# The first MLP of a four-layer attention kernel written by token, with its norm and modulation on ACT from the fifth group on

## The chip, the cores and the metric

The kernel runs on one core of a Trainium2 chip. A core has five engines that run beside each other, each with its own instruction queue: PE (matrix multiply; its loads of stationary operands are listed apart as PEld), DVE (vector), ACT (scalar, with the activation functions), POOL (a slower vector engine[...]) and SP, which here only issues DMAs. Instructions of one engine start in program order; engines wait for each other through semaphores. Matrix products land in PSUM, everything else lives in SBUF. The metric is the time of one execution on the device in microseconds (us). The kernel before takes 1635.25 us, the median of 3 runs (1635.12 to 1635.38).

## The reference, cut to what matters

`x` is 128 batches of 64 tokens of 128 channels in float32, `ctx` has the same shape, `cond` is one vector of 128 per batch. Four layers follow each other. Layers 0 and 2 have a self-attention, a cross-attention to `ctx` and an MLP; layer 1 is a cross-attention, layer 3 a routed mixture of experts. The change is in the MLP of layer 0 and in the statistics of `ctx` that layers 1 and 2 need:

```python
mod = silu(cond) @ adaln_w + adaln_b          # six vectors of 128 per batch
sh_sa, sc_sa, g_sa, sh_ff, sc_ff, g_ff = split(mod, 6)
...
xm = layernorm(x, 1e-6) * (1 + sc_ff) + sh_ff # the MLP's input
h  = gelu(xm @ fc1_w + fc1_b)                 # 512 hidden channels
x  = x + g_ff * (h @ fc2_w + fc2_b)
# layer 1: layernorm(x, 1e-5), layernorm(ctx, 1e-5);  layer 2: layernorm(ctx, 1e-6)
```

## The kernel before, in words

The 8192 tokens are cut into 16 groups of 512 tokens (8 batches). A group's `x` stays in SBUF for the whole kernel as `xs[s]`, 128 tokens per partition row in four tiles. All order is written out by hand: the program order of the Python calls is the order in each engine's queue, and so in SP's queue of DMAs.

**Attention** (`attend`) is a software pipeline of half groups. Each `step(k)` emits the scores of one half (PE, then on DVE the row maximum L477 and the subtraction L479, 2.3 us each), the transposes and exponentials of the half before, the weighted sum of the half before that, and pieces of `prepare` (norm, keys, queries, values of groups to come) and `finish` (normalise, project, add to `x`).

**The first MLP** (`mlp` called with `mv_out=x_mv`) runs 18 turns. For group `j`, `turn(j)` emits, in this order: the norm of group j+2 (`norm`: five POOL instructions, L361 and four of L364); four products into the 512 hidden channels (`hidden`, PE L676, and Gelu on ACT, L677), each followed by one of the four products out of them for group j-1 (`output`, L682); between the second and third of these `enter`, which transposes the normed group j+1 on PE (L334), multiplies it with its scale on DVE (L339) and adds its shift on POOL (L340); `measure`, the statistics of group j+3 on DVE (L312, L314) and their inverse root on POOL (L321, L322); then `beside(j)`, which loads and measures context group j (`measure_context`: one DMA, eight DVE instructions, seven POOL instructions L654 to L657) and computes one piece of the tables of later layers; last `gate(j-1)` (bias and gate on DVE, L707) and `leave(j-2)`, which transposes the product back to tokens (PE, L715), adds it to `x` (DVE, L716) and takes the statistics of the new `x` for layer 1.

The product `py` of the first MLP comes out with channels on partitions, hence the transposes of L715. The MLP of layer 2 is called with `by_token=True`: there the hidden activations are the stationary operand (L692), `py` has tokens on partitions, and bias and gate come from a tile `gt` that two DMAs per group broadcast from a small table in DRAM (`gate_table`, `gate_tile`); POOL adds the bias part (L698), DVE multiplies with the gate (L702) and adds (L703).

**The seams.** `into_mlp` interleaves the MLP's first five pieces (`heads`) and its first turns with the last steps of the attention before. At the other end, five turns are followed by pieces of the next attention's `prepare` (`second` in `stages`), which add norms and masked keys (L364, L403, L436) to POOL's queue; the last products of group 15 and the first scores of the next attention come after them.

Of the kernel before, what the change touches and what calls it, by code (L numbers as in the profile page):

```python
# [9 lines left out]
F32 = mybir.dt.float32  # L10
AF = mybir.ActivationFunctionType
# [48 lines left out]
def tile_kernel(ctx: ExitStack, tc: tile.TileContext, a: dict, out: bass.AP):  # L60
# [5 lines left out]
    def const(shape, name):  # L66
        return cp.tile(shape, F32, tag=name, name=name)
# [231 lines left out]
    def by_batch(t):  # L299
        return t.rearrange("p (b l) -> p b l", b=NB)  # L300


    ctx_rs = {eps: const([P, NST, TT], f"ctx_rs{i}") for i, eps in enumerate((1e-5, 1e-6))}
    ctx_nb = {eps: const([P, NST, TT], f"ctx_nb{i}") for i, eps in enumerate((1e-5, 1e-6))}


    x_mv = const([P, NST, TT, 2], "x_mv")
# [70 lines left out]
    def prepare(pools, at):  # L378
# [16 lines left out]
        if cross:  # L395
            cn = c
            if layer != "L0c":
                cn = pool.tile([P, TT, P], F32, tag="cn", name="cn", bufs=1)
                for t in range(TT):
                    rs, nb = (v[eps][:, s, t : t + 1] for v in (ctx_rs, ctx_nb))  # L400

                    if layer == "L1c" or s == 0:
                        G.tensor_scalar(cn[:, t, :], c[:, t, :], rs, nb, ALU.mult, ALU.add)  # L403
                    else:
                        S.activation(cn[:, t, :], c[:, t, :], AF.Identity, bias=nb, scale=rs)
# [238 lines left out]

    def measure_context(s):
        pool = pools[0]
        c = pool.tile([P, TT, P], F32, tag="cm", name="c")
        nc.sync.dma_start(c, ctx_d[s])  # L650
        mv = pool.tile([P, TT, 2], F32, tag="mvc", name="mvc")
        stats(pool, c, mv)
        nmu = pool.tile([P, TT], F32, tag="nmuc", name="nmuc")
        G.tensor_scalar(nmu, mv[:, :, 0], -1.0, 0.0, ALU.mult, ALU.add)  # L654
        for eps in ctx_rs:
            rs = power(ctx_rs[eps][:, s], mv, eps)
            G.tensor_tensor(ctx_nb[eps][:, s], nmu, rs, ALU.mult)  # L657

    def mlp(wmod, w1, b1, w2, b2, beside, mv_out=None, by_token=False):

        pool, psum = pools[:2]

        def measure(d):
            d["mv"], d["rs"] = stats_of(pool, xs[d["s"]], 1e-6)

        def norm(d):
            d["xn"] = normed_by_pool(pool, xs[d["s"]], d["mv"], d["rs"], "xn")

        def enter(d):
            d["xm"] = modulated(pool, transposed(psum, d["xn"]), wmod, 4, 3, d["s"])  # L670

        def hidden(d, f):
            if f == 0:
                d["h"] = pool.tile([P, 4, NT], F32, tag="e", name="h")
            ph = pools[2].tile([P, 512], F32, tag="ph", name="ph")
            T.matmul(ph, w[w1][:, 0, ts(f, P)], d["xm"], start=True, stop=True)  # L676
            S.activation(d["h"][:, f, :], ph, AF.Gelu_apprx_tanh, bias=col(b1, f))  # L677

        def output(d, f):
            if f == 0:  # L680
                d["py"] = pools[3].tile([P, 512], F32, tag="py", name="py")
            T.matmul(d["py"], w[w2][:, f, :], d["h"][:, f, :], start=f == 0, stop=f == 3)  # L682

        def gates_of(d):
            d["gt"] = gate_tile(pool, d["s"], w2)

        def output_by_token(d, t):
# [9 lines left out]
        def bias_by_token(d):  # L697
            G.tensor_tensor(xs[d["s"]], xs[d["s"]], d["gt"][:, :, 1, :], ALU.add)  # L698

        def leave_by_token(d):  # L700
            y = pool.tile([P, TT, P], F32, tag="y", name="y")
            V.tensor_tensor(y, d["py"], d["gt"][:, :, 0, :], ALU.mult)  # L702
            V.tensor_add(xs[d["s"]], xs[d["s"]], y)  # L703

        def gate(d):
            d["y"] = pool.tile([P, NT], F32, tag="y", name="y")
            V.scalar_tensor_tensor(  # L707
                by_batch(d["y"]), by_batch(d["py"]), col(b2), mod(wmod, 5, d["s"]),
                ALU.add, ALU.mult,
            )  # L710

        def leave(d):
            pt = psum.tile([P, 512], F32, tag="mm", name="psB")
            for t in range(TT):
                T.transpose(pt[:, ts(t, P)], d["y"][:, ts(t, P)], ident)  # L715
            V.tensor_add(xs[d["s"]], xs[d["s"]], pt.rearrange("p (t c) -> p t c", t=TT))  # L716
# [16 lines left out]

        def turn(j):
            out = output_by_token if by_token else output
            go(norm, j + 2)
            go(hidden, j, 0)
            go(out, j - 1, 0)
            go(hidden, j, 1)
            go(out, j - 1, 1)  # L740
            go(enter, j + 1)
            go(measure, j + 3)
            if by_token:
                go(bias_by_token, j - 1)
            go(hidden, j, 2)
            go(out, j - 1, 2)
            if 0 <= j < NST:
                beside(j)
            go(hidden, j, 3)
            go(out, j - 1, 3)  # L750
            if by_token:
                go(leave_by_token, j - 1)
                go(gates_of, j)
            else:
                go(gate, j - 1)
                go(leave, j - 2)

        return heads, [lambda j=j: turn(j) for j in range(NST + 2)]


# [412 lines left out]
    def stages():  # L1173
# [4 lines left out]
            pools, [attention_of(s, layer) for layer in ("L1c", "L2s", "L2c") for s in groups]  # L1178
        )

        def beside_0(j):
            measure_context(j)
            if j < len(later_tables):
                later_tables[j]()

        def beside_2(j):
# [2 lines left out]

        heads_0, turns_0 = mlp(  # L1190
            "L0_xcond_adaln_w", "L0_xcond_fc1_w", "L0_xcond_fc1_b", "L0_xcond_fc2_w",
            "L0_xcond_fc2_b", beside_0, mv_out=x_mv,
        )
        heads_2, turns_2 = mlp(
            "L2_xcond_W_mod", "L2_xcond_W_mlp1", "L2_xcond_b_mlp1", "L2_xcond_W_mlp2",
            "L2_xcond_b_mlp2", beside_2, by_token=True,
        )
        last = 5

# [32 lines left out]
            f()  # L1232
        first_mods[2]()
        n = last + 2 + len(heads_0)
        for f in steps_1[6:-n]:
            f()
        rest = into_mlp(steps_1, heads_0, turns_0)
        second = [(0, 1, 2), (0,), (1, 0), (0, 0, 1, 2), (0, 1, 1, 2, 0, 0, 3, 3)]
        n_ = len(second)
# [66 lines left out]
```

## Time and profile before

| | us |
|---|---|
| median of 3 runs | 1635.25 |
| the profiled execution: time of the run | 1632.74 |
| its span from first to last instruction | 1631.0 |
| first MLP, first hidden product (turn 0) | at 408.07 |
| turns 0 to 3 | 408.07 to 443.44 |
| turns 4 to 13 | 443.44 to 523.53 |
| turns 14 to 16 with the next attention's first pieces | 523.53 to 557.06 |
| second MLP, turn 0 starts | at 1136.03 |

The profile lists for each instruction its start, its length, and, in brackets, how long its engine had stood idle before it and which instruction of which engine ended that. PE is busy for nearly the whole span, so a change counts by what it takes from PE's queue or adds to it, and by the gaps in it. The granted PE clock is 0.996 over the span. There are three stretches of 3.4 us at half clock, one near the start, one from 557.4 us (the end of the first MLP) and one from 1130.8 us.

### The profile page before, as it was taken

The numbers are of one execution on the slowest core, as the hardware profiler recorded it, in microseconds if no ns is written. First come the engines' busy times: TensorE is split into PE (matmuls) and PEld (weight loads), VectorE is DVE, ScalarE is ACT, GpSimd is POOL, SyncE is SP. The second block draws the span as 40 slices with busy tenths as digits, with TensorE's granted clock in tenths as the row PEclk, the third lists the DMA queues.
The fourth block names the chain that finished last, engine by engine and source line by source line (L and its number), as shares of the span: only waits on it lengthen the run. The fifth ranks groups of instructions, "written<-read, shape, count | busy, mean of one in ns | idle before, by whom it ended". The sixth has DMA issues, their size and how long they took to land.

```text
span 1631.0 us, 64964 instructions
## 1 busy us (share of the span) xinstructions
PE 1577.1 (97%) x27842; PEld 1089.0 (67%) x27842; DVE 1296.5 (79%) x2430; ACT 1037.2 (64%) x1710; POOL 1084.7 (67%) x1818
## 2 busy tenths in 40 slices
PE   6999999998999899999999999998999999999998
PEld 4677777776554477777777677776777666666665
DVE  7999999998576688899999999997454576666666
ACT  5788777776333587788888888886334544444443
POOL 6688776776799888986778876665876333333322
PEclk9999999999999999999999999999999999999999
DMA  7334443322202022211333532222433111111100
GB/s 208 82 82 97 108 121 91 89 80 62 61 27 59 27 58 62 63 47 49 85 94 82 116 95 63 73 57 57 120 91 78 30 39 37 40 33 35 34 11 20
DMA packets 146783, 112.71 MB, mean 69 GB/s; under 512 B 36357, under 2 KB 125247, under 8 KB 146495
## 3 DMA queue, kind: packets, MB, share of 16 engines
q1 hardware_dynamic: 146288, 108.53, 25.8%
q8 instruction: 219, 3.59, 1.0%
q14 instruction: 69, 0.57, 0.1%
q10 hardware_dynamic: 207, 0.03, 0.0%
HBM read 83.99 MB, written 14.02 MB: 60 GB/s over the span
## 4 chain that ended last, share of the span: by engine, by line
PE 79%; DVE 13%; ACT 3%; POOL 3%; issue 1%; DMA 0%; SPq 0%; POOLq 0%; DVEq 0%; ACTq 0%
PE sc L470 10%; PE pp L495 9%; PE po L512 7%; PE ph L1063 6%; PE ph L1064 6%; DVE e L479 6%; DVE mx L477 6%; PE ph L676 6%; PE po L1094 5%; PE psT L334 5%; PE pk L428 5%; PE py L555 4%; PE py L692 3%; PE pvv L451 3%; PE pq L441 3%; PE py L682 2%
## 5 line engine op out<-in xcount | busy, mean ns | idle before, releaser
L499 ACT ACTIVATE eT<-pp 128x1024 f32<-128x1024 f32 x320 | 329.8, 1030 | 159.4 <-PE pp L495 159.3
L477 DVE TENSOR_REDUCE mx<-sc 128x32 f32<-128x2048 f32 x160 | 366.6, 2291 | 58.6 <-PE sc L470 58.6
L479 DVE TENSOR_TENSOR e<-sc,mx 128x2048 f32<-128x2048 f32 x160 | 366.6, 2291 | 5.4
L495 PEld LDWEIGHTS pp<-ident,e 64*128 64x128 f32 x5120 | 184.9, 139 | 140.7 <-ACT eT L499 44.8
L495 PE MATMUL pp<-ident,e 64*128 64x64 f32 x5120 | 228.7, 229 | 7.1 <-DVE e L479 4.7
L364 POOL TENSOR_SCALAR xn<-x,nmu,rs 128x128 f32<-128x128 f32 x508 | 224.7, 456 | 13.3
L436 POOL TENSOR_SCALAR kbd<-kT,mask 128x512 f32<-128x512 f32 x316 | 213.2, 693 | 26.9 <-ACT kT L430 24.5
L549 POOL TENSOR_TENSOR oT<-o,rb 128x512 f32<-128x512 f32 x80 | 102.3, 1278 | 164.5 <-DMA rb<-recs 63.6
L470 PE MATMUL sc<-kbd,qT 32*64 32x256 f32 x5120 | 180.5, 389 | 16.4 <-DVE e L479 15.4
L677 ACT ACTIVATE h<-ph,vec 128x512 f32<-128x512 f32 x128 | 87.4, 688 | 154.8 <-PE ph L676 154.6
L512 PE MATMUL po<-eT,vbd 128*32 128x64 f32 x10240 | 178.4, 221 | 1.1 <-issue 1.0
L1070 ACT ACTIVATE h<-h 128x512 f32<-128x512 f32 x112 | 70.6, 630 | 148.1 <-DVE h L1066 129.2
L512 PEld LDWEIGHTS po<-eT,vbd 128*32 128x32 f32 x10240 | 151.9, 110 | 14.0 <-issue 1.6
L322 POOL TENSOR_TENSOR rs<-rs,nhalf 128x4 f32<-128x4 f32 x128 | 130.4, 1019 | 10.7
L470 PEld LDWEIGHTS sc<-kbd,qT 32*64 32x64 f32 x5120 | 98.1, 131 | 53.1 <-issue 20.2
L1066 DVE TENSOR_TENSOR h<-ph,ab 128x512 f32<-128x512 f32 x112 | 77.0, 688 | 56.2 <-PE ph L1064 56.1
L312 DVE BATCH_NORM_STATS2 st<-x 128x6 f32<-128x128 f32 x512 | 110.5, 278 | 0.8 <-DMA x<-in_x_dram 0.3
L1099 DVE SCALAR_TENSOR_TENSOR acc<-po,pr,acc 128x128 f32<-128x128 f32 x192 | 67.3, 350 | 44.1 <-PE po L1094 39.5
L1063 PE MATMUL ph<-nx,w 128*128 128x512 f32 x192 | 99.9, 602 | 0.0
L520 ACT COPY o<-po 128x512 f32<-128x512 f32 x160 | 95.8, 598 | 5.2 <-PE po L512 3.6
L1064 PE MATMUL ph<-u,w_ev 128*128 128x512 f32 x192 | 98.0, 592 | 0.0
L1094 PEld LDWEIGHTS po<-w_2o,h 128*128 128x128 f32 x768 | 92.1, 192 | 8.7 <-issue 8.4
(261 smaller groups left out, 2849.8 us busy)
## 6 DMA issues: line engine op xcount, KB each, us to landing
rb<-recs SPq DMA_DIRECT2D x80, 256.0 KB
c<-in_ctx_dram SPq DMA_DIRECT2D x64, 256.0 KB
o<-o SPq DMA_DIRECT2D x320, 32.0 KB
gt<-gate_L_xcond_sa_proj_w SPq DMA_DIRECT2D x32, 256.0 KB
gt<-gate_L_xcond_W_proj SPq DMA_DIRECT2D x32, 256.0 KB
gt<-gate_L_xcond_W_mlp SPq DMA_DIRECT2D x32, 256.0 KB
x<-in_x_dram SPq DMA_DIRECT2D x16, 256.0 KB
ctxT<-cm SPq DMA_DIRECT2D x16, 256.0 KB
```

The source lines that it names most:

```text
L322: G.tensor_tensor(rs, rs, nhalf, ALU.pow)
L364: engine.tensor_scalar(xn[:, t, :], src[:, t, :], nmu[:, t : t + 1], rs[:, t : t + 1], ALU.add, ALU.mult)
L436: (V if at.get("first") else G).tensor_scalar(kbd[:, j], by_batch(kT), mask[:, j : j + 1], 1.0, ALU.mult, ALU.mult)
L470: T.matmul(sc[ts(h, L), g, ts(t2, 256)], qT[ts(g, 32), ts(b, L)], kbd[ts(g, 32), :, b, :], start=True, stop=True,)
L477: V.tensor_reduce(mx, sc.rearrange("p g (m k) -> p (g m) k", k=L), AX.X, ALU.max)
L479: V.tensor_tensor(e, sc.rearrange("p g (m k) -> p (g m) k", k=L), mx.unsqueeze(2).broadcast_to([P, 32, L]), ALU.subtract,)
L495: T.transpose(pp[:, h, ts(4 * g2 + 2 * i + t2, L)], e6[ts(h, L), 2 * gg + g2, t2, i], ident[ts(h, L), ts(h, L)],)
L499: S.activation(eT[:, gg], pp, AF.Exp, scale=HD ** -0.5)
L512: T.matmul(po[ts(g, 32), i, ts(2 * t2 + h, L)], at["vbd"][:, 4 * u + 2 * t2 + h, 2 * g + i, :], e7[:, g // 2, h, g % 2, i, t2, :], start=T ...
L1063: T.matmul(ps, wn, d["nx"], start=True, stop=False)
L1064: T.matmul(ps, we, d["u"], start=False, stop=True)
L1094: T.matmul(po[:, ex, :], d[q][:, ts(t, P)], k3["w_2o"][:, q, :], start=r == 0, stop=r == 1)
```

## The change

Six things are edited.

1. The first MLP is written like the second: `output`, `bias`, `leave` by token. The variants with channels on partitions go (`gate`, the transposes of L715). `leave(j-1)` follows the products of group j-1 in the same turn, and the statistics for layer 1 follow it. Each turn issues the two DMAs of `gate_tile` for the next group, which wait behind what SP has queued before.
2. The table that these read is made in steps 7 and 9 of the first attention, one DVE product in the one, two PE transposes, one DVE copy and a DMA in the other.
3. For groups 4 to 15 (`by_act=4`), `norm` is two small POOL instructions (the bias `-mean/std`) and four ACT instructions, and `enter` uses `modulated_by_batch`, eight ACT instructions on 64 columns each, instead of one DVE and one POOL instruction.
4. Contexts are loaded ahead: groups 0 and 1 beside the last two `heads`, then group s+2 right after the statistics of group s are issued.
5. No context is measured in turns 0 to 3; turns 4, 6, 8 and 10 measure two each, turns 5, 7, 9 and 11 to 15 one.
6. One context's POOL part is five instructions instead of seven: both powers are one instruction over 8 columns, and so are both products.

```diff
     def measure_context(s):
         pool = pools[0]
-        c = pool.tile([P, TT, P], F32, tag="cm", name="c")
-        nc.sync.dma_start(c, ctx_d[s])
         mv = pool.tile([P, TT, 2], F32, tag="mvc", name="mvc")
-        stats(pool, c, mv)
+        stats(pool, measured[s], mv)
+        load_context(s + 2)
         nmu = pool.tile([P, TT], F32, tag="nmuc", name="nmuc")
         G.tensor_scalar(nmu, mv[:, :, 0], -1.0, 0.0, ALU.mult, ALU.add)
-        for eps in ctx_rs:
-            rs = power(ctx_rs[eps][:, s], mv, eps)
-            G.tensor_tensor(ctx_nb[eps][:, s], nmu, rs, ALU.mult)
+        rs = ctx_rs[:, s]
+        for i, eps in enumerate(ctx_eps):
+            G.tensor_scalar(rs[:, i], mv[:, :, 1], eps, 1.0, ALU.add, ALU.mult)
+        G.tensor_tensor(rs, rs, nhalf.unsqueeze(1).broadcast_to([P, 2, TT]), ALU.pow)
+        G.tensor_tensor(ctx_nb[:, s], nmu.unsqueeze(1).broadcast_to([P, 2, TT]), rs, ALU.mult)
...
         def norm(d):
-            d["xn"] = normed_by_pool(pool, xs[d["s"]], d["mv"], d["rs"], "xn")
+            if d["s"] < by_act:
+                d["xn"] = normed_by_pool(pool, xs[d["s"]], d["mv"], d["rs"], "xn")
+                return
+            nb = pool.tile([P, TT], F32, tag="nmuxn", name="nb")
+            G.tensor_scalar(nb, d["mv"][:, :, 0], -1.0, 0.0, ALU.mult, ALU.add)
+            G.tensor_tensor(nb, nb, d["rs"], ALU.mult)
+            d["xn"] = pool.tile([P, TT, P], F32, tag="xn", name="xn")
+            for t in range(TT):
+                S.activation(
+                    d["xn"][:, t, :], xs[d["s"]][:, t, :], AF.Identity,
+                    bias=nb[:, t : t + 1], scale=d["rs"][:, t : t + 1],
+                )
 
         def enter(d):
-            d["xm"] = modulated(pool, transposed(psum, d["xn"]), wmod, 4, 3, d["s"])
+            f = modulated if d["s"] < by_act else modulated_by_batch
+            d["xm"] = f(pool, transposed(psum, d["xn"]), wmod, 4, 3, d["s"])
...
         def turn(j):
-            out = output_by_token if by_token else output
             go(norm, j + 2)
             go(hidden, j, 0)
-            go(out, j - 1, 0)
+            go(output, j - 1, 0)
             go(hidden, j, 1)
-            go(out, j - 1, 1)
+            go(output, j - 1, 1)
             go(enter, j + 1)
             go(measure, j + 3)
-            if by_token:
-                go(bias_by_token, j - 1)
+            go(bias, j - 1)
             go(hidden, j, 2)
-            go(out, j - 1, 2)
+            go(output, j - 1, 2)
             if 0 <= j < NST:
                 beside(j)
             go(hidden, j, 3)
-            go(out, j - 1, 3)
-            if by_token:
-                go(leave_by_token, j - 1)
-                go(gates_of, j)
-            else:
-                go(gate, j - 1)
-                go(leave, j - 2)
+            go(output, j - 1, 3)
+            go(leave, j - 1)
+            go(gates_of, j)
...
+        contexts = iter(groups)
+
         def beside_0(j):
-            measure_context(j)
+            for _ in range(0 if j < 4 else 2 if j in (4, 6, 8, 10) else 1):
+                measure_context(next(contexts))
             if j < len(later_tables):
                 later_tables[j]()
...
-        for f in steps_1[6:-n]:
-            f()
+        table = in_two(
+            gate_table, "L0_xcond_adaln_w", "L0_xcond_fc2_w", 5, col("L0_xcond_fc2_b")
+        )
+        for k, f in enumerate(steps_1[6:-n]):
+            f((), [table[k // 2]] if k in (1, 3) else ())
+        for s in range(2):
+            heads_0[3 + s] = lambda s=s, f=heads_0[3 + s]: (f(), load_context(s))
```

More of the change, by code (lines that the diff above doesn't have):

```diff
@@ L300, in by_batch @@
         return t.rearrange("p (b l) -> p b l", b=NB)
-    ctx_rs = {eps: const([P, NST, TT], f"ctx_rs{i}") for i, eps in enumerate((1e-5, 1e-6))}
-    ctx_nb = {eps: const([P, NST, TT], f"ctx_nb{i}") for i, eps in enumerate((1e-5, 1e-6))}
+    ctx_eps = (1e-5, 1e-6)
+    ctx_rs, ctx_nb = (const([P, NST, 2, TT], n) for n in ("ctx_rs", "ctx_nb"))
     x_mv = const([P, NST, TT, 2], "x_mv")
@@ L399, in prepare @@
                 for t in range(TT):
-                    rs, nb = (v[eps][:, s, t : t + 1] for v in (ctx_rs, ctx_nb))
+                    rs, nb = (v[:, s, ctx_eps.index(eps), t : t + 1] for v in (ctx_rs, ctx_nb))
                     if layer == "L1c" or s == 0:
@@ L643, in attention_of, with load_context, mlp @@
         )
+    measured = {}
+    def load_context(s):
+        if s < NST:
+            measured[s] = pools[0].tile([P, TT, P], F32, tag="cm", name="c")
+            nc.sync.dma_start(measured[s], ctx_d[s])
     def measure_context(s):
         pool = pools[0]
-        c = pool.tile([P, TT, P], F32, tag="cm", name="c")
-        nc.sync.dma_start(c, ctx_d[s])
         mv = pool.tile([P, TT, 2], F32, tag="mvc", name="mvc")
-        stats(pool, c, mv)
+        stats(pool, measured[s], mv)
+        load_context(s + 2)
         nmu = pool.tile([P, TT], F32, tag="nmuc", name="nmuc")
         G.tensor_scalar(nmu, mv[:, :, 0], -1.0, 0.0, ALU.mult, ALU.add)
-        for eps in ctx_rs:
-            rs = power(ctx_rs[eps][:, s], mv, eps)
-            G.tensor_tensor(ctx_nb[eps][:, s], nmu, rs, ALU.mult)
-    def mlp(wmod, w1, b1, w2, b2, beside, mv_out=None, by_token=False):
+        rs = ctx_rs[:, s]
[3 more added lines that the diff above has]
+        G.tensor_tensor(ctx_nb[:, s], nmu.unsqueeze(1).broadcast_to([P, 2, TT]), rs, ALU.mult)
+    def mlp(wmod, w1, b1, w2, beside, mv_out=None, by_act=NST):
         pool, psum = pools[:2]
@@ L677, in hidden, with output @@
             S.activation(d["h"][:, f, :], ph, AF.Gelu_apprx_tanh, bias=col(b1, f))
[L679 to L682, printed above, removed]
         def gates_of(d):
             d["gt"] = gate_tile(pool, d["s"], w2)
-        def output_by_token(d, t):
+        def output(d, t):
             if t == 0:
@@ L695, in output_by_token, with bias, leave @@
                 )
-        def bias_by_token(d):
+        def bias(d):
             G.tensor_tensor(xs[d["s"]], xs[d["s"]], d["gt"][:, :, 1, :], ALU.add)
-        def leave_by_token(d):
+        def leave(d):
             y = pool.tile([P, TT, P], F32, tag="y", name="y")
@@ L703, in leave_by_token @@
             V.tensor_add(xs[d["s"]], xs[d["s"]], y)
[L705 to L716, printed above, removed]
             if mv_out is not None:
@@ L1191, in stages @@
             "L0_xcond_adaln_w", "L0_xcond_fc1_w", "L0_xcond_fc1_b", "L0_xcond_fc2_w",
-            "L0_xcond_fc2_b", beside_0, mv_out=x_mv,
+            beside_0, mv_out=x_mv, by_act=4,
         )
@@ L1195, in stages @@
             "L2_xcond_W_mod", "L2_xcond_W_mlp1", "L2_xcond_b_mlp1", "L2_xcond_W_mlp2",
[L1196 removed]
+            beside_2,
         )
```

## The prediction, made before the change was run

> **What bounds the kernel now.** I read the page first (which engine is full), then the first MLP by stretches, then PE's order of time there for its gaps, then the queues behind the gaps. PE is the full engine:
>
> ```profile
> PE 1577.1 (97%) x27842; PEld 1089.0 (67%) x27842; DVE 1296.5 (79%) x2430; ACT 1037.2 (64%) x1710; POOL 1084.7 (67%) x1818
> ```
>
> In the windows of turns 4 to 13 of the first MLP and of turns 2 on of the second (length, then busy us of PE, PEld, DVE, ACT, POOL), PE stands still for 0.8 of 80.09 us, but POOL is 91% busy; the second MLP, already by token, has no PE gap at all:
>
> ```profile
> 443.44:523.53 80.09, 79.27 (x255) 39.70 (x255) 54.70 (x272) 27.51 (x40) 72.60 (x153) 1.00 0.15 43
> 1149.57:1265.40 115.83, 115.83 (x723) 86.97 (x722) 56.55 (x189) 44.03 (x64) 83.99 (x137) 1.00 0.39 98
> ```
>
> PE's gaps (in brackets) are POOL's modulation arriving late at turns 2, 4 and 14, and at the end the first scores of the next attention:
>
> ```profile
> 425.14 1.13 PE L676 MATMUL ph<-xm,L_xcond_fc_w 128*128 128x512 f32 x2 [2.62 <-POOL xm L340]
> ...
> 443.44 1.13 PE L676 MATMUL ph<-xm,L_xcond_fc_w 128*128 128x512 f32 x2 [0.76 <-POOL xm L340]
> ...
> 523.53 1.12 PE L676 MATMUL ph<-xm,L_xcond_fc_w 128*128 128x512 f32 x2 [0.81 <-POOL xm L340]
> ...
> 557.06 1.77 PE L470 MATMUL sc<-kbd,qT 32*64 32x256 f32 x32 [2.48 <-DVE e L479]
> ```
>
> POOL's queue, one context block: 3.4 us from L654 to the next L361, of which the two powers are 2 x 1.09 (start to next start). Without power the same shape takes 0.20.
>
> ```profile
> 426.47 0.20 POOL L654 TENSOR_SCALAR nmuc<-mvc 128x4 f32<-128x4 f32 x1
> 426.72 0.20 POOL L321 TENSOR_SCALAR ctx_rs<-mvc 128x4 f32<-128x4 f32 x1
> 427.01 1.01 POOL L322 TENSOR_TENSOR ctx_rs<-ctx_rs,nhalf 128x4 f32<-128x4 f32 x1
> 428.09 0.20 POOL L657 TENSOR_TENSOR ctx_nb<-nmuc,ctx_rs 128x4 f32<-128x4 f32 x1
> ```
>
> **What PE gains.** (a) The three gaps, 2.62+0.76+0.81 = 4.2: without contexts, turns 0 to 3 have the second MLP's queues, whose turn 2 starts 13.54 after turn 0; with two tables of 0.44 that is 14.4, against 17.07 here. (b) A turn without a table lasts 7.74 (451.74 to 459.48); the second MLP's lasts 7.44 (1149.57 to 1157.01): the transposes (0.44) go, products by token are 0.13 dearer. Fourteen turns give 14 x 0.30 = 4.2; for groups 14 and 15 the transposes lie under DVE already, so only 2 x 0.13 is lost. Net 3.9. Gain 8.1.
>
> **What is added and hidden, or nearly.** The table (a DVE product 0.29 and copy 0.39, two transposes 0.22) falls where PE and DVE take turns as limit: 0 to 0.7, I take 0.4. ACT does four norms in 1.65 and eight pieces of modulation in 2.48; with four Gelus (2.5) 6.6 of a 7.44 turn. It fits only if it never waits. No table load appears between Gelu and L351 at 530 to 535. The 32 gate DMAs are those of the second MLP, where the bias L698 never waited for one. The context loads of groups 0 and 1 go ahead of the finish DMAs on SP, 0.55 each, while SP waits for DVE anyway; without that cover 1.1. Later loads wait on SP for the statistics two contexts earlier, with the gate DMAs behind; these are issued by 8.3 and wanted some 6 us later.
>
> ```profile
> 970.07 1.65 ACT L405 ACTIVATE cn<-c,ctx_nb,ctx_rs 128x128 f32<-128x128 f32 x4
> ...
> 542.53 2.48 ACT L351 ACTIVATE cm<-psT,mod_L_xcond_Wss_kv 128x64 f32<-128x64 f32 x8 [0.17 <-PE psT L334]
> ```
>
> **The new wait: ACT behind POOL's double contexts.** POOL gets one bias per turn (1.25) and keeps the root of group j+3 (1.3). Then come the contexts, and only then, first in turn j+1, the pair (0.55) that ACT needs for norm j+3. On ACT two Gelus and the modulation of group j+2 queue behind that norm, and PE opens turn j+2 with it. A context block is now 0.26+0.28+0.28+power+0.27. The trace has no power over 8 columns: if it is paid per instruction, 1.09, block 2.2; if per column, (1.02-0.20)/4 = 0.205, so 1.84+0.08, block 3.0. Its nearest row says that 4 columns of anything else cost 0.20, so I take 3.0 and keep both.
>
> Durations for this, start to next start in the rows: DVE product and addition 0.63 each (L702, L703: 0.69 alone), statistics of one group 1.06 (L312 with L314), root 1.3 (L321 with L322), bias 1.25 (L698), a norm on POOL 2.06. PE's last product of a turn ends with the turn, DVE sees it 0.2 later. In us from the start of turn 4: DVE multiplies group 2's gate (0.2 to 0.84), adds it (to 1.47), takes its statistics (2.53), adds to the last `x` of the attention (3.2), measures group 7 (4.2). POOL: root 4.35 to 5.65, bias 6.9, two blocks 12.9, pair 13.45. The turn lasts 7.88, so 5.6 into turn 5. There ACT needs 1.55+0.61+0.61+2.35+0.2 = 5.3: modulation at 10.95, PE wanted it at 7.44. Stall **3.5** (block 2.2: 1.85). While PE stalls, DVE and POOL go on, so POOL takes up turn 6's root at 0.7 instead of 3.75; its pair comes 2.1 into turn 7, the modulation at 7.55, PE wants it at 7.58. Turn 8 as turn 4, without the last `x`: 3.75+1.3+1.25+6.0+0.55 = 12.85, 5.2 into turn 9, modulation 10.6 against 7.66 (a table's transposes lie in turn 9): **2.95** (1.5). Turn 10 as turn 6. Single turns end 2.3 into the next, 7.6 against 7.44 to 7.66: 0.6 in all (0). Turn 12 has a root for the next attention (1.3): turn 13 stalls **1.25** (0.65). Sum 8.3 (4.0).
>
> **The new wait at the end.** Today DVE takes y, x, statistics and then the first maximum without a pause, while POOL is still at it at 555:
>
> ```profile
> 549.89 0.75 DVE L707 SCALAR_TENSOR_TENSOR y<-py,vec,mod_L_xcond_adaln_w 128x512 f32<-128x512 f32 x1 [6.02 <-PE py L682]
> 550.55 0.68 DVE L716 TENSOR_TENSOR x<-x,psB 128x512 f32<-128x512 f32 x1
> 551.26 0.87 DVE L312 BATCH_NORM_STATS2 st<-x 128x6 f32<-128x128 f32 x4
> 552.05 0.36 DVE L314 BATCH_NORM_AGGREGATE x_mv<-st 128x2 f32<-128x6 f32 x4
> 552.33 2.26 DVE L477 TENSOR_REDUCE mx<-sc 128x32 f32<-128x2048 f32 x1
> ```
>
> Now DVE's addition for group 15 needs POOL's bias of 15, last in POOL's queue. From the start of turn 12: POOL ends the pair for 15 at 11.15, bias 12 12.4, context 15.4, root 16.7, norm and context of the next attention's first group (2.06+1.75) 20.5, bias 13 21.75, context 24.75. It then waits for DVE's product for that group's queries (27.15), adds 28.35, norms group 1 32.15, root 33.45, bias 14 34.7, context 37.7, keys (2.7) 40.4, addition 41.5, group 2 45.3, root 46.6, bias 15 **47.85**. Turns 12 and 13 with the stalls above take 7.64+8.9, turn 14 with two sets of transposes 8.7, turn 15 7.0, the attention's pieces 5.5 (540.61 to 546.15) and group 15's products 3.7: PE finishes at 41.45 if nothing more holds it, and the maximum would start at 43.85 (2.4 later, as now). Bias 14 at 34.7 holds DVE's leave of 14, and behind it the product whose PSUM slot the next query projection waits for (0.85 already today), so PE by 1.8; bias 15 holds the maximum to 47.95+0.63+1.06 = 49.65. Loss **5.8** (block 2.2: 4.9). Behind the held addition stand maximum and subtraction; the next scores wait for these.
>
> **Sum.** 8.1-0.4-8.3-5.8 = -6.4: the profiled execution's 1632.74 (span 1631.0 and 1.7 around it) becomes 1639.1. The median of the runs lies 2.5 above it, so **1641.7**. With the cheap block 8.1-0.4-4.0-4.9 = -1.2.
>
> [...] DVE's new addition has two SBUF inputs, which L716 (one from PSUM) had not. Its row in the second MLP is 0.69, but once
>
> ```profile
> 1158.19 1.75 DVE L703 TENSOR_TENSOR x<-x,y 128x512 f32<-128x512 f32 x1 [0.29 <-POOL x L698]
> ```
>
> while POOL worked. [...] By the row's median nothing. I take 0. [...] Here the 2.48 gap was followed by half clock (32 score products in 1.77, not 1.12; about 1.5 with what follows), the 2.33 gap at 402 by none. [...] I take 0. Both speak against the change; the upper end keeps 5.
>
> **Rivals.** *Cheap power*: as worked, about +1.2, 1636.5. For it: one instruction instead of two is all that the trace can't price. *POOL block still cheaper, ends faster*: the loss falls by (6.4-1.2)/0.8 = 6.5 per us of block, so from 1.5 us down (all five instructions near 0.3, power of 8 columns in a queue hardly dearer than a multiply) the kernel is 3.3 faster, 1632; at 1.4, 1631.3. For it: the powers are always measured behind the addition that feeds them. Against it: L657, fed by the power in the same way, takes 0.20. [...] *ACT does not relieve POOL* because its norm waits on POOL for the pair: that is my main case.
>
> **How the numbers follow.** Main case 0.5, cheap power 0.24, port and clock 0.1, faster 0.16. Measurement can tell about 0.2%, 3.3 us, from no change: slower 0.6, within 0.24, faster 0.16. The range goes from 1630.5 (half of the faster case) to 1647.5; the main case's own is 1638.5 to 1645.
>
> **What would show it.** Right: PE gaps before L676 at the starts of turns 6 and 10 ended by ACT's modulation; ACT's norm waiting for POOL's pair; DVE's addition of group 15 waiting for POOL's bias by over 3 us; turns 0 to 3 without gaps. Wrong: a power over 8 columns near 1.0, or POOL idle when turn 16 comes.

## The result, and the profile after

The changed kernel takes 1640.49 us (median of six runs, 1638.48 to 1642.9) against 1635.18 for the kernel before, measured beside it: ratio **1.0037**, 95% interval 1.0026 to 1.0048. A second set of runs gave 1.0033 (1.002 to 1.0046). So it is slower by 5.4 to 6.0 us by these ratios (5.3 by the two medians), where 1641.7 was predicted. The profiled execution takes 1642.14 (span 1640.3); before it took 1632.74 (span 1631.0).

The first row of the page says that PE has the same work, ACT 43 us more than before and POOL 20 less:

```profile
PE 1577.9 (96%) x28164; PEld 1119.9 (68%) x28164; DVE 1290.4 (79%) x2420; ACT 1080.0 (66%) x1854; POOL 1065.1 (65%) x1754
```

Nothing in it says "slower". The windows of the first MLP do. These are turns 0 to 3, turns 4 to 13, and from turn 14 to the second set of scores of the next attention; columns as in the prediction, with the granted clock after POOL:

```profile
411.48:443.10 31.62, 31.27 (x244) 23.01 (x240) 17.63 (x69) 17.66 (x34) 21.38 (x32) 1.00 0.39 95
443.10:527.21 84.11, 78.83 (x455) 58.35 (x455) 53.38 (x297) 63.44 (x161) 63.45 (x120) 0.98 0.47 120
527.21:565.67 38.46, 28.39 (x207) 20.62 (x207) 16.96 (x59) 20.46 (x48) 33.54 (x64) 0.88 0.19 48
```

Before, the same three stretches took 35.37, 80.09 and 33.53. The front gained 3.75, the middle lost 4.02 although POOL fell from 72.60 to 63.45 busy us there, and the end lost 4.93. In the middle PE now stands still for 5.3 of 84.1 us while no engine is full. PE's order of time shows where and for whom:

```profile
443.10 1.12 PE L698 MATMUL ph<-xm,L_xcond_fc_w 128*128 128x512 f32 x2 [0.35 <-ACT xm L351]
...
460.26 1.12 PE L698 MATMUL ph<-xm,L_xcond_fc_w 128*128 128x512 f32 x2 [1.56 <-ACT xm L351]
...
493.88 1.12 PE L698 MATMUL ph<-xm,L_xcond_fc_w 128*128 128x512 f32 x2 [2.31 <-ACT xm L351]
...
527.21 1.12 PE L698 MATMUL ph<-xm,L_xcond_fc_w 128*128 128x512 f32 x2 [1.06 <-ACT xm L351]
...
548.28 2.08 PE L441 MATMUL pq<-xm,L_xcond_Wq 128*128 128x512 f32 x2 [3.18 <-DVE xm L339]
...
565.67 2.01 PE L470 MATMUL sc<-kbd,qT 32*64 32x256 f32 x32 [6.55 <-DVE e L479]
```

The gap of turn 2 (2.62, POOL) is gone. Those of turns 4 and 14 have changed their releaser from POOL to ACT, and turns 6 and 10 have got new ones (turn 8 a small one of 0.34). ACT is only a messenger. The first line is its largest wait from turn 0 to the second scores (us in all, times, longest), the others are its queue in turn 5:

```profile
ACT xn L685 <- POOL nb L682: 22.4, 9, 4.4
```

```profile
455.06 1.65 ACT L685 ACTIVATE xn<-x,nb,rs 128x128 f32<-128x128 f32 x4 [3.97 <-POOL nb L682]
456.61 1.24 ACT L699 ACTIVATE h<-ph,vec 128x512 f32<-128x512 f32 x2
457.75 2.46 ACT L351 ACTIVATE xm<-psT,mod_L_xcond_adaln_w 128x64 f32<-128x64 f32 x8
```

The modulation that PE needs (457.75) stands behind a norm that is wanted a turn later and that waited 3.97 us for POOL. POOL's queue from turn 4 into turn 5 shows what it was doing, two context blocks and then the pair, as the prediction calls the two small operations that make `nb`:

```profile
448.87 0.20 POOL L661 TENSOR_SCALAR nmuc<-mvc 128x4 f32<-128x4 f32 x1
449.13 0.45 POOL L664 TENSOR_SCALAR ctx_rs<-mvc 128x4 f32<-128x4 f32 x2
449.66 1.65 POOL L665 TENSOR_TENSOR ctx_rs<-ctx_rs,nhalf 128x8 f32<-128x8 f32 x1
451.39 0.20 POOL L666 TENSOR_TENSOR ctx_nb<-nmuc,ctx_rs 128x8 f32<-128x8 f32 x1
451.56 0.20 POOL L661 TENSOR_SCALAR nmuc<-mvc 128x4 f32<-128x4 f32 x1
...
454.54 0.19 POOL L681 TENSOR_SCALAR nb<-mv 128x4 f32<-128x4 f32 x1
454.82 0.20 POOL L682 TENSOR_TENSOR nb<-nb,rs 128x4 f32<-128x4 f32 x1
```

A block is 2.69 us (448.87 to 451.56), and the power over 8 columns takes 1.65, against 1.01 over 4 columns: between the two bounds of the prediction. At the end, DVE's order of time:

```profile
556.61 0.69 DVE L719 TENSOR_TENSOR y<-py,gt 128x512 f32<-128x512 f32 x1 [8.39 <-PE py L709]
559.14 0.69 DVE L720 TENSOR_TENSOR x<-x,y 128x512 f32<-128x512 f32 x1 [1.84 <-POOL x L715]
559.87 0.87 DVE L312 BATCH_NORM_STATS2 st<-x 128x6 f32<-128x128 f32 x4
560.66 0.36 DVE L314 BATCH_NORM_AGGREGATE x_mv<-st 128x2 f32<-128x6 f32 x4
560.94 2.26 DVE L477 TENSOR_REDUCE mx<-sc 128x32 f32<-128x2048 f32 x1
```

DVE's product of group 15 is followed by a wait for POOL's bias, and the first maximum, and so the scores at 565.67, stand behind it. Group 14 met the same (545.77, a wait of 2.25), and its statistics stand ahead of the product that the query projection at 548.28 waits for. On POOL the two biases (L715) stand behind an addition (L340) that waits for DVE:

```profile
538.31 1.04 POOL L340 TENSOR_TENSOR xm<-xm,mod_L_xcond_Wss_q 128x512 f32<-128x512 f32 x1 [3.03 <-DVE xm L339]
...
544.48 1.26 POOL L715 TENSOR_TENSOR x<-x,gt 128x512 f32<-128x512 f32 x1
...
549.03 2.70 POOL L436 TENSOR_SCALAR kbd<-kT,mask 128x512 f32<-128x512 f32 x4
...
557.84 1.27 POOL L715 TENSOR_TENSOR x<-x,gt 128x512 f32<-128x512 f32 x1
```

From 538.31 to 559.11 POOL works without a pause, so bias 15 comes when everything ahead of it in the queue is done. For the loads of contexts and gates, which the change moves too, no engine waits in these stretches.

### The profile page after: what moved, and what is told of

It is laid out like the page before. It is cut to its first block, busy times and chain, and to the rows that moved or that the text cites. A ratio compares the mean times of both kernels' runs of the same rounds, so it can differ in the third digit from the quotient of the medians.

```text
span 1640.3 us, 65757 instructions
## 1 busy us (share of the span) xinstructions
PE 1577.9 (96%) x28164; PEld 1119.9 (68%) x28164; DVE 1290.4 (79%) x2420; ACT 1080.0 (66%) x1854; POOL 1065.1 (65%) x1754
## 4 chain that ended last, share of the span: by engine, by line
PE 74%; DVE 12%; ACT 4%; POOL 4%; DMA 3%; issue 2%; SPq 0%; POOLq 0%; DVEq 0%
PE sc L470 9%; PE pp L495 8%; PE po L512 6%; PE ph L1061 6%; PE ph L1062 6%; PE ph L698 5%; PE po L1092 5%; DVE mx L477 5%; PE py L709 5%; DVE e L479 5%; PE psT L334 4%; PE pk L428 4%; PE py L555 4%; PE pvv L451 3%; PE pq L441 3%; DMA rb<-recs 2%
## 5 line engine op out<-in xcount | busy, mean ns | idle before, releaser
L436 POOL TENSOR_SCALAR kbd<-kT,mask 128x512 f32<-128x512 f32 x316 | 213.0, 693 | 37.2 <-ACT kT L430 34.9
L364 POOL TENSOR_SCALAR xn<-x,nmu,rs 128x128 f32<-128x128 f32 x460 | 202.8, 456 | 12.0
L549 POOL TENSOR_TENSOR oT<-o,rb 128x512 f32<-128x512 f32 x80 | 102.1, 1277 | 161.0 <-DMA rb<-recs 46.8
```

Source lines behind the costliest of these rows:

```text
L364: engine.tensor_scalar(xn[:, t, :], src[:, t, :], nmu[:, t : t + 1], rs[:, t : t + 1], ALU.add, ALU.mult)
L436: (V if at.get("first") else G).tensor_scalar(kbd[:, j], by_batch(kT), mask[:, j : j + 1], 1.0, ALU.mult, ALU.mult)
```

## The experiments

The theory: the loss is the **order in POOL's queue**, at two places: the pair for ACT's norm behind two context blocks, and the biases of groups 14 and 15 behind the next attention's pieces. Rivals: ACT's own work, by token as such, POOL's amount of work, the clock. The times of a group of runs share one measurement of the kernel before, so ratios are compared across groups. Where lines are inserted, line numbers behind them move by 1 or 2.

**The changed kernel again**, for a second trace, since in the first one a DMA in the middle of the first attention landed late (3.4 us at 206 us).

> The changed kernel once more, for a second trace. Theory 1 (order of POOL's queue): the gaps of PE before the first product of turns 6, 10 and 14 and before the query projection and the first scores at the end recur within 0.5 us (1.56, 2.31, 1.06, 3.18, 6.55), ratio to before again about 1.004. The 3.4 us lost at 206 us in the first attention (a DMA that landed late) is taken as an accident of one execution and should be gone. Rival: it recurs, and is then a part of the loss that belongs to the change.

1639.95 us, ratio 1.0033 (1.002 to 1.0046). The late DMA did not come again here: the end of the first attention (the transposes behind PE's gap of 2.33) begins at 404.79, where it began at 408.08 in the first trace and at 404.67 before, and at 403.03 to 406.70 in the later traces: an accident of one execution, and no part of the change. The gaps came again to within 0.03 us (0.34, 1.57, 0.34, 2.31, 1.07, then 3.21), except for the last one, 7.38 instead of 6.55. What didn't come again is the half clock in turn 10. The first trace has, behind the gap of 2.31,

```profile
493.88 1.12 PE L698 MATMUL ph<-xm,L_xcond_fc_w 128*128 128x512 f32 x2 [2.31 <-ACT xm L351]
494.84 1.46 PE L709 MATMUL py<-L_xcond_fc_w,h 128*128 128x128 f32 x8
496.09 1.91 PE L698 MATMUL ph<-xm,L_xcond_fc_w 128*128 128x512 f32 x2
```

and the second, behind the same gap,

```profile
492.19 1.13 PE L698 MATMUL ph<-xm,L_xcond_fc_w 128*128 128x512 f32 x2 [2.31 <-ACT xm L351]
493.15 1.05 PE L709 MATMUL py<-L_xcond_fc_w,h 128*128 128x128 f32 x8
494.04 1.02 PE L698 MATMUL ph<-xm,L_xcond_fc_w 128*128 128x512 f32 x2
```

so turns 4 to 13 take 82.47 here, not 84.11. The second trace is the better measure of the queues, and it is used below.

**The pair first.**

```
 def measure(d):
     d["mv"], d["rs"] = stats_of(pool, xs[d["s"]], 1e-6)
+    if d["s"] >= by_act:
+        d["nb"] = nb = pool.tile([P, TT], F32, tag="nmuxn", name="nb")
+        G.tensor_scalar(nb, d["mv"][:, :, 0], -1.0, 0.0, ALU.mult, ALU.add)
+        G.tensor_tensor(nb, nb, d["rs"], ALU.mult)
 def norm(d):
     ...
-    nb = pool.tile([P, TT], F32, tag="nmuxn", name="nb")
-    G.tensor_scalar(nb, d["mv"][:, :, 0], -1.0, 0.0, ALU.mult, ALU.add)
-    G.tensor_tensor(nb, nb, d["rs"], ALU.mult)
+    nb = d["nb"]
```

> The two small POOL operations that ACT's norm waits for (the negated mean times the root) are issued right behind that group's root, ahead of the bias and of the context blocks, for groups 4 to 15. Theory 1: ACT's waits for POOL in the first MLP (22 us in all) go, and with them PE's gaps at turns 4 to 14 (0.35+1.56+0.34+2.31+1.06 = 5.6) and the half clock after turn 10 (1.65): turns 4 to 13 take about 77 us instead of 84.1. At the end nothing is mended: if POOL is ahead there, about 7 us faster than the changed kernel, 1633.5; if POOL's queue as a whole sets the end (rival 1: too much work on POOL, in whatever order), PE only arrives earlier at the same bias of group 15, the gap before the first scores grows from 6.5 to 12 or so, and the time stays within 2 us of 1640.5. Rival 2 (ACT is too full with 6.6 of 7.44 us a turn, or by-token products are dearer): the gaps stay, no change.

1632.42 us, ratio **0.9987** (0.9979 to 0.9996): 7.5 us faster than the changed kernel run beside it. Not one PE gap over 0.3 us is left in turns 0 to 14, and turns 4 to 13 are PE's work and nothing else (75.99 of 75.99); the end is unchanged:

```profile
442.52:518.51 75.99, 75.99 (x457) 56.87 (x455) 53.75 (x295) 63.44 (x158) 62.38 (x118) 1.00 0.51 132
```

```profile
539.49 1.58 PE L441 MATMUL pq<-xm,L_xcond_Wq 128*128 128x512 f32 x2 [3.20 <-DVE xm L339]
...
556.89 2.01 PE L470 MATMUL sc<-kbd,qT 32*64 32x256 f32 x32 [7.37 <-DVE e L479]
```

ACT has the same 63.44 busy us in both, so its amount of work was not the limit. Nor does POOL's amount set the end: PE comes to it some 7 us earlier from the start of the MLP, and the gaps there are 3.20 and 7.37 as before (3.21 and 7.38).

**The bias of groups 14 and 15 on DVE**, alone and with the pair first.

```
 def bias(d):
-    G.tensor_tensor(xs[d["s"]], xs[d["s"]], d["gt"][:, :, 1, :], ALU.add)
+    late = mv_out is not None and d["s"] >= NST - 2
+    (V if late else G).tensor_tensor(
+        xs[d["s"]], xs[d["s"]], d["gt"][:, :, 1, :], ALU.add
+    )
```

> The bias of groups 14 and 15 of the first MLP is added by DVE instead of POOL, nothing else. Theory 1: DVE no longer waits for POOL there (2.25 and 1.84), PE's gap before the query projection falls from 3.2 to about 0.9 and that before the first scores from 6.5 to about 3, with 1 to 2 us less at half clock: 5 us faster than the changed kernel, about 1635.5. Rival 1 (the end is set by DVE's own work, two more additions of 0.65 on it): no change or 1 us slower. Turns 4 to 13 are as in the changed kernel by all theories.

> Both edits together. Theory 1: the gains add, 10 to 12 us faster than the changed kernel, 1629 to 1631, which is 4 to 6 faster than before. Rival 1 (POOL has too much work in all between turns 4 and 15): the sum is no better than the second edit alone, about 1635. Rival 2 (ACT): as the second edit alone too, but with gaps ended by ACT at turns 6 and 10.

Alone: 1635.93 us, ratio 1.0002 (0.9992 to 1.0011), 4.0 faster than the changed kernel. Both: 1629.04, ratio 0.9965 (0.9952 to 0.9977), 10.9 faster; 7.5 and 4.0 make 11.5, so the two places add up. Alone, the end reads

```profile
541.93 1.12 PE L441 MATMUL pq<-xm,L_xcond_Wq 128*128 128x512 f32 x2 [0.97 <-DVE xm L339]
...
555.31 2.02 PE L470 MATMUL sc<-kbd,qT 32*64 32x256 f32 x32 [2.52 <-DVE e L479]
```

with turns 4 to 13 at 82.47 as in the changed kernel. From the start of turn 14 to the first maximum it takes 27.51 instead of 33.78. Of these 6.3 the medians keep 3.4 to 4.0. In both traces 0.85 is given back up to the third maximum. With both edits the scores and the three sets of products behind them (550.83 to 556.87) take 6.04, with the pair first alone (556.89 to 561.88) 4.99, at full clock 3.40: more of them are at half clock behind the gap of 2.52 than behind the one of 7.37. Where the rest goes stays open: over all runs the granted clock is not lower with the bias on DVE, in the mean 0.9951 against 0.9944 without it, and with the pair first 0.9940 against 0.9937.

**One context per turn**, from turn 0.

```
-    for _ in range(0 if j < 4 else 2 if j in (4, 6, 8, 10) else 1):
-        measure_context(next(contexts))
+    measure_context(j)
```

> One context is measured in each turn 0 to 15 (as before the change), with the loads ahead, the one power over 8 columns and ACT's norm kept; the pair that ACT's norm waits for stays where it is, behind the context block. Theory 1 (a pair behind two blocks is late, behind one it is not): the gaps before turns 6, 10 and 14 go (1.56, 2.31, 1.06), as in the changed kernel's turns with one block (0 to 0.35), so turns 4 to 13 take 76 to 77 us instead of 82.5 to 84; turns 0 to 3, where POOL has its norm, the addition of the modulation, the root, the bias and now a block, lose their gain: 34.5 to 36 instead of 31.6. The end (6.2 us of it) is as in the changed kernel. Sum about 3 faster than the changed kernel, 1637. Rival (the pair is late behind any block, since what holds it is its place and not the block's length): the gaps stay with one block, at 1 to 2 us in every turn, and the kernel is slower than the changed one.

1639.7 us, ratio 1.0049 (1.0033 to 1.0066): not the 3 us faster than the changed kernel that had been expected, and by the ratios rather slower (1.0037 and 1.0033; the intervals overlap). The queue did what the theory says: no gap over 0.3 from turn 5 to turn 13, with the pair still in its place behind one block. Turns 0 to 3 take 35.12 (34.5 to 36 expected). What was missed is turn 4:

```profile
445.08 2.07 PE L698 MATMUL ph<-xm,L_xcond_fc_w 128*128 128x512 f32 x2 [3.44 <-ACT xm L351]
...
525.63 1.12 PE L698 MATMUL ph<-xm,L_xcond_fc_w 128*128 128x512 f32 x2 [1.26 <-ACT xm L351]
```

POOL comes out of turns 0 to 3 late, the first of ACT's norms finds its pair late, and the gap of 3.44 is followed by half clock: the first three sets of products behind it take 2.07, 1.92 and 1.91 instead of 1.12, 1.05 and 1.02, and turn 4 takes 10.70 instead of 7.99. So the double blocks are not wrong in themselves: they buy the front, and cost it back only through the place of the pair, as the pair first shows, which has the double blocks and no gap.

**POOL's norm for all groups**, with the double contexts (`by_act` left out, first) and with one per turn (second, with the edit of the experiment before as well; of the change, the products by token, their tables, the earlier loads and the shorter block are left).

```
-    beside_0, mv_out=x_mv, by_act=4,
+    beside_0, mv_out=x_mv,
```

> All groups of the first MLP are normed and modulated by POOL and DVE (as groups 0 to 3), the contexts as in the changed kernel. Theory 1 (POOL is the engine that the change fills): in turns 4 to 13 POOL has per turn a norm with its mean 2.2 to 2.5, a root 1.3, a bias 1.25, an addition of the modulation 1.04, and 1.2 blocks of 2.7: about 9.2 us against PE's 7.66, so these ten turns take some 91 us instead of 82.5, and the kernel is 8 slower than the changed one, about 1648. Rival (ACT with its 6.6 us a turn is the limit): without them the gaps ended by ACT go and nothing comes in their place, 5 faster, 1635.

> By token alone: POOL's norm for all groups and one context per turn 0 to 15, so of the change only the products by token, the bias and gate tables and the context block of five operations are left. Theory 1: POOL has in each of turns 0 to 13 about 8.7 us (2.3 + 1.3 + 1.25 + 1.04 + 2.7) against PE's 7.5: turns 0 to 13 take about 121 us, instead of 114 to 116 in the changed kernel and 115.5 before; the end as in the changed kernel. About 1646. Rival (by token is a gain in itself, 0.22 to 0.3 per turn): 1633.

1652.66 us, ratio 1.013 (1.0116 to 1.0144), and 1649.97, ratio 1.0115 (1.0099 to 1.013): both slower than any other version, by 21.5 and 18.9 against before where 13 and 11 had been expected. Turns 4 to 13 of the first and of the second:

```profile
439.06:535.51 96.45, 82.41 (x456) 60.31 (x454) 59.12 (x306) 27.48 (x40) 87.36 (x156) 0.95 0.39 104
```

```profile
442.59:530.96 88.37, 78.64 (x454) 57.61 (x455) 53.75 (x274) 27.50 (x40) 82.58 (x143) 1.00 0.39 102
```

In the second, every turn from 4 to 12 lasts 8.68 to 8.71, whatever PE has in it: that is POOL's sum (8.7 expected), and turns 0 to 13 take 122.36 (121 expected). In the first they take 96.45 from turn 4 on where 91 was written down, with 0.95 of the clock granted over them and half clock behind a gap of 3.42 (at 476.53, where the first three sets of products take 2.08, 1.92 and 1.92). What both expectations left out is the end: from turn 14 to the first maximum it takes 37.2 in both, 3.4 more than in the changed kernel, since the late POOL goes into it late. So by token without ACT's norm would be 19 us slower than before: 6.9 in turns 0 to 13 (122.36 against 115.46), 8.4 up to the first maximum (37.2 against 28.8), the rest not located. ACT does relieve POOL, in amount.

**Longer and shorter context blocks**, in the changed kernel: two powers over 4 columns, and one power left out.

```
-        G.tensor_tensor(rs, rs, nhalf.unsqueeze(1).broadcast_to([P, 2, TT]), ALU.pow)
+        for i in range(2):
+            G.tensor_tensor(rs[:, i], rs[:, i], nhalf, ALU.pow)
```

```
-        G.tensor_tensor(rs, rs, nhalf.unsqueeze(1).broadcast_to([P, 2, TT]), ALU.pow)
+        G.tensor_tensor(rs[:, 0], rs[:, 0], nhalf, ALU.pow)
```

> The changed kernel with two powers over 4 columns per context (2 x 1.09) in place of one over 8 (1.73 from start to start): a block of 3.14 us on POOL instead of 2.69. Theory 1 (a double block delays the pair by twice what a block grows): the gaps before turns 6 and 10 grow by 0.9 each to 2.5 and 3.2, before turn 14 by 0.45 to 1.5, those of the single turns by 0.3: 3 us slower than the changed kernel, up to 3 more where half clock follows the two longer gaps. The end does not change. About 1643.5 (ratio to before 1.0055). Rival (length of the blocks does not matter): no change.

> The changed kernel with the power over 4 of the 8 columns only: the root of the second epsilon is left out, so that what uses it is scaled by the variance instead of its inverse root; a block of 2.05 us instead of 2.69, near the cheap block of the prediction. Theory 1: the gap before turn 6 falls by 1.3 to 0.3, before turn 10 to 1.0, before turn 14 to 0.4, the single turns to 0: 3.9 faster than the changed kernel, about 1636.6 (ratio to before 1.001), which is what the prediction gave for the cheap power. The end keeps its 3.2 and 6 to 7. Rival (POOL's amount of work sets the end too): the gap before the first scores falls by 1 to 2 as well, 1635.

With two powers 1644.31 us, ratio 1.0076 (1.0061 to 1.009); with one less 1634.74, ratio 1.0011 (1.0001 to 1.002); 1.0055 and 1.001 had been expected. The gaps of the first, and then of the second:

```profile
459.87 2.08 PE L699 MATMUL ph<-xm,L_xcond_fc_w 128*128 128x512 f32 x2 [2.43 <-ACT xm L351]
...
495.19 1.13 PE L699 MATMUL ph<-xm,L_xcond_fc_w 128*128 128x512 f32 x2 [2.77 <-ACT xm L351]
```

```profile
471.56 1.12 PE L698 MATMUL ph<-xm,L_xcond_fc_w 128*128 128x512 f32 x2 [1.01 <-ACT xm L351]
...
503.70 1.12 PE L698 MATMUL ph<-xm,L_xcond_fc_w 128*128 128x512 f32 x2 [1.52 <-ACT xm L351]
```

Turns 4 to 13 take 85.90, 82.47 and 79.57 with blocks of 3.05 (two powers: 447.63 to 450.68 in that trace), 2.69 and about 2.05. The gaps of turns 4 to 14 make 7.3, 5.6 and 2.9 in sum: a longer block costs more, though not quite the 3 us more and 3.9 less that were expected (with two powers 1.5 of the 3.4 us is half clock in turn 6, whose first two sets of products take 2.08 and 1.67 instead of 1.12 and 1.05). The places were not as expected: with the short block the gaps of turns 6 and 10 vanish, but turns 8 and 12, which had 0.34 and none, get 1.01 and 1.52. In turn 5 of that trace POOL's root of group 8 waited 1.70 us for ACT's norm, which still reads the root's buffer: the two queues hold each other. That this wait is what moves the gaps was not tried. The end keeps its two gaps, 3.16 and 6.73, but from turn 14 to the first maximum it takes 32.96 with the short block and 34.05 with two powers, against 33.78: one block stands between the two biases in POOL's queue (from bias 14 to bias 15 it is 12.73, 13.71 and 13.40). So what sets the end is what is ahead of the bias in the queue, its length included.

**The bias of groups 14 and 15 early on POOL**, with the pair first.

```
 def turn(j):
+    early = mv_out is not None and j >= NST - 2
+    if early:
+        go(gates_of, j)
     ...
-    go(bias, j - 1)
+    if mv_out is None or j - 1 < NST - 2:
+        go(bias, j - 1)
     ...
     go(leave, j - 1)
-    go(gates_of, j)
+    if early:
+        go(bias, j)
+    else:
+        go(gates_of, j)
```

> The pair first, and the bias of groups 14 and 15 stays on POOL, but goes ahead of the next attention's pieces: at the end of its own turn instead of the middle of the next, with the gate tile of these two groups loaded at the start of the turn. Theory 1 (DVE at the end waits for the bias's place in POOL's queue, behind an addition of the modulation that itself waits for DVE, and not for the amount of POOL's work): the gaps before the query projection and the first scores are as with the bias on DVE (1.0 and 2.5), 1628 to 1630. Rival (POOL's amount of work sets the end, the bias on DVE helped by taking 2.5 us off POOL): no better than the pair first alone, 1632 to 1633.

1623.51 us, ratio **0.9954** (0.9942 to 0.9967), which is 1627.7 on the scale of the first measurement, where 1628 to 1630 had been expected. POOL's bias of group 14 now stands ahead of the addition that waits for DVE, in time that was idle:

```profile
525.04 1.27 POOL L717 TENSOR_TENSOR x<-x,gt 128x512 f32<-128x512 f32 x1
526.80 1.04 POOL L340 TENSOR_TENSOR xm<-xm,mod_L_xcond_Wss_q 128x512 f32<-128x512 f32 x1 [0.49 <-DVE xm L339]
```

The query projection waits 1.04 and the scores 2.71, and it is 27.46 from turn 14 to the first maximum: POOL has the same work as in the changed kernel, only in another order, and all of the 6.3 is back. What cost it was the order and not the amount.

**DVE's statistics of groups 14 and 15 later**, on top of that.

```
 def leave(d):
     ...
-    if mv_out is not None:
-        stats(pool, xs[d["s"]], mv_out[:, d["s"]])
+    if mv_out is not None and d["s"] < NST - 2:
+        measure_out(d)
 def turn(j):
+    if mv_out is not None and j >= NST:
+        go(measure_out, j - 2)
```

> The pair first, the early bias, and DVE's statistics of the sums of groups 14 and 15 (1.06 each, wanted only by the last groups of the next attention) moved behind the product for the query projection and behind the first maximum and subtraction. Theory 1 (at the end DVE's order is what is left): the gap before the query projection falls from 1.04 to about 0, that before the first scores from 2.71 to 1.65, below any gap after which half clock was seen: 2.1 faster than with the pair first and the early bias, 3 to 4 where the half clock goes too, ratio to before 0.993 to 0.994. Rival (another wait, POOL's norm of the context at 0.95, takes its place): 1 us or less.

1623.31 us, ratio 0.9940 (0.9927 to 0.9953). From turn 14 to the first maximum it takes 26.05 instead of 27.46, but the two intervals overlap, so the edit's worth is not shown by the times. The expected size was not reached: the query projection still waits 0.85 and the scores 1.39, with a wait of 1.09 for POOL's context norm between the two, the wait that the rival had named:

```profile
535.35 1.12 PE L441 MATMUL pq<-xm,L_xcond_Wq 128*128 128x512 f32 x2 [0.85 <-DVE xm L339]
...
544.52 1.62 PE L334 MATMUL psT<-ident,cn 128*128 128x128 f32 x4 [1.09 <-POOL cn L403]
...
547.52 1.12 PE L470 MATMUL sc<-kbd,qT 32*64 32x256 f32 x32 [1.39 <-DVE e L479]
```

## Why the prediction was right, step by step

| step | predicted | measured | from |
|---|---|---|---|
| gaps of turns 2, 4, 14 and the shorter turns, turns 0 to 13 | +8.4 | +8.37 | 35.37 + 80.09 before, 31.10 + 75.99 with the pair first |
| two table steps in the first attention | -0.4 | -0.14 | in nine of the twelve traces with the tables one maximum of the first attention is 0.42 later than before and the next 0.28 earlier |
| ACT behind POOL's double contexts | -8.3 (-4.0 cheap) | -6.99 | 31.61 + 82.47 in the changed kernel again, less 107.09 |
| end, from turn 14 to the first maximum, net | -5.8 - 0.3 | -4.98 | 33.78 changed (again), 28.80 before |
| sum | -6.4 | -3.7 | |

**Gains** came out as worked. With the new waits taken away, the turns from 5 to 12 last 7.44 to 7.67, which are the 7.44 taken from the second MLP with and without a table's transposes.

**The table steps** cost less than the 0.4 taken, and inside its bounds.

**ACT behind POOL** was right in its mechanism and its places (turns 6 and 10, then 14); the sizes were too large, 3.5, 2.95 and 1.25 against 1.56, 2.31 and 1.06 before turns 6, 10 and 14, and the largest gap is that of turn 10 and not of turn 6. Two terms of the working were off. The power over 8 columns took 1.65, and the block 2.69, not 3.0. And "PE's last product of a turn ends with the turn, DVE sees it 0.2 later" fails in turn 3: PE has the attention's last output products (L555, 1.06) and the gap of 0.35 behind it, so DVE began group 2's gate 1.20 before turn 4 (441.90 against 443.10), and POOL's root came 3.27 into the turn instead of 4.35. These 1.08, with 0.33 for the two blocks (5.67 from 448.87 to 454.54, not 6.0; the second holds a power of 1.94) and 0.12 for root, bias and pair, bring the pair 1.53 earlier; with turn 5 beginning 0.11 and wanting its successor 0.17 later than worked, and ACT's way of 5.24 instead of 5.3, 3.5 falls to 1.6. The gaps' own brackets (5.6 in sum) are less than the 6.99 that the turns lost: a turn that ends in a gap is longer by the bracket and 0.17 more, and the one behind it by 0.1.

**The end** was right in both holds: bias 14 to the query projection (1.8 more than before predicted, 3.18 - 0.85 = 2.3 measured), bias 15 to the first maximum. Bias 15 was to end 47.85 after the start of turn 12; it ended at 559.11 - 510.75 = 48.4. Its working rests on POOL's wait for DVE's product of the first queries (27.15 predicted, 538.31 - 510.75 = 27.6 measured), and on the work ahead of the bias from there on, not on how full POOL was before, and the pair first shows that: PE came early, the whole chain moved with it. One sign was missed: DVE's addition of group 15 was to wait for the bias by over 3 us and waited 1.84 and 2.67 in the two traces, because PE came late to these products as well: from the query projection to their end it took 8.2 and 7.4 us, partly at half clock (0.50 granted from 546.5 to 553.4 in the first trace; the 32 products of L451 took 1.98 in both, 1.15 with both edits), where it takes 5.9 with the bias early. What was mis-sized is the sentence on groups 14 and 15, "only 2 x 0.13 is lost": turn 14 gained 1.36 (9.68 to 8.32 with the pair first), since it too had transposes of 0.44 before, and its context transposes waited for POOL's norm inside (1.15 instead of 0.60 for the four). Without this gain the new holds cost 6.3 (5.8 predicted), by the bias early or on DVE (27.46 and 27.51).

**The rest.** 3.7 of the 5.4 to 6.0 us are in the table. Behind the first maximum the changed kernel loses 0.3 to 0.6 more in two half-steps (12.55 from the first to the third maximum before, 13.18 and 12.81 in the two traces), the half clock behind the long gap (0.50 granted for 6.83 us from 563.6 in the first trace, where the 32 score products took 2.01 instead of 1.12). The other 1 to 2 us are not located: from the third maximum to the second MLP one trace takes 0.2 more than before and the other 2.5, so single executions of one and the same kernel differ by as much. That the total came out within 2 us of 1641.7 is thus in part luck: the located loss is 3.7 and not 6.4, and losses that were not worked out make up for part of the difference.

**The clock** was taken as 0 with up to 3 kept for the upper end. It costs 1.66 in turn 10 of one trace (0.50 granted for 3.41 us from 495.3) and nothing in the other, and is part of the end in both (0.88 and 0.91 granted over it, 1.00 before). Whether a gap of about 2.3 to 2.8 is followed by it differs from trace to trace, as the last section shows, so neither 0 nor a loss in every execution was the right term. **DVE's addition beside POOL**, taken at its row's median, was right where it mattered: the addition took 0.69 to 0.72 from turn 4 to the end of this MLP. It was longer once, in turn 3, where it began 0.35 behind an operation of POOL on two SBUF tiles:

```profile
434.45 1.28 POOL L549 TENSOR_TENSOR oT<-o,rb 128x512 f32<-128x512 f32 x1
434.80 1.48 DVE L720 TENSOR_TENSOR x<-x,y 128x512 f32<-128x512 f32 x1
```

No run shows the 5 us that the range keeps for these two at its upper end, nor the loss that the chance of 0.1 for port and clock stands for: the runs showed 1.66 for half clock in turn 10 of one trace, its part in the end, and this one addition 0.79 longer.

**Rivals.** The cheap power was given 1636.5; with one power left out and a block of 2.05 the ratio is 1.0011, 1637 on the prediction's scale. ACT relieves POOL (1652.66 without its norm), so what makes the changed kernel slow is not the amount of its work but who stands ahead of whom.

## What to carry to other kernels

When work goes from a full engine to an idle one, list what the idle engine still needs from the full one and put that ahead in the full one's queue: two operations of 0.2 us behind two blocks of 2.7 cost 7 us here, and moving them up, with the biases put ahead of an addition that itself waits, made a kernel that was 0.33 to 0.37% slower than the one before 0.46% faster, with no work taken away. A busy time that falls (POOL's from 72.6 to 63.5 us in the middle) is no sign of a gain; what counts is where in the queue the wanted result stands.

## What the runs showed of the hardware

**Half clock followed some gaps and not others of the same length.** In the changed kernel's first trace 0.50 is granted for 3.41 us from 27.7, 205.2 and 495.3 and for 6.83 us from 546.5 and 563.6; in the kernel before for 3.41 us from 28.3, 557.4 and 1130.8 (besides a stretch at the very end of each). The distances between these starts are 52, 85, 15 and 5 times 3.413 us in the one and 155 and 168 times in the other. The gap of 2.33 us at the end of the first attention is in all thirteen traces; half clock followed it in nine (in the changed kernel again the eight products of L555 then took 2.04 instead of 1.16). That of 2.31 in turn 10 was followed by it in one trace of three. With two powers a gap of 2.43 was followed by it (two products in 2.08) and one of 2.77 was not (1.13); in the kernel before, the 2.48 was (32 score products in 1.77 instead of 1.12) and the 2.62 of turn 2 was not (two products in 1.13). The two stretches of 6.83 began inside the gaps of 3.18 and 6.55, and behind the gaps of 3.42 and 3.44 in turns of the MLP two products took 2.08 and 2.07. No half clock followed the gap of 2.18 before turn 4 by token alone (1.12), nor the 1.94 and 1.73 with POOL's norm for all groups (1.13 and 1.12). What decides between these was not tried.

**DVE's addition of two SBUF tiles beside POOL.** In the changed kernel's first trace it took 0.69 in 26 of 32 cases, also in six that began 0.44 to 1.32 us behind a power over 8 columns that was still running (459.56, 469.06, 476.72, 492.44, 511.77 and 519.22). It took 1.48 and 1.74 in the two that began 0.35 and 0.08 behind POOL's product L549 (434.80 and 1167.67), and 0.73 to 0.80 in three that began 0.19 to 0.26 behind a piece of POOL's norm, L364 (1198.83, 1207.81 and 1252.22). Some POOL operations that began during an addition were longer too: one over 4 columns took 0.69 instead of 0.20 (545.83, begun 0.06 behind the addition at 545.77), one over 8 columns 0.73 instead of 0.20 (484.80, 0.03 behind), and a power over 8 columns 1.94 instead of 1.65 (452.35, 0.26 behind); these three additions kept 0.69 to 0.72.

**A power on POOL** takes 1.01 over 4 columns and 1.65 over 8: neither one price per instruction nor one per column; a straight line through these two points would be 0.37 and 0.16 per column, an estimate.
